# A two-layer graph network on one core: an addition at the ring's lap becomes a copy on ScalarE, and the last groups use four PSUM banks

## The chip, the cores and the metric

The kernel runs on one core of a Trainium2 chip. The metric is the device time of one execution in microseconds (us). The engines are named as in the profile: PE (TensorE), DVE (VectorE), ACT (ScalarE), POOL (GpSimd) and SP (SyncE, which here only issues DMAs).

## The reference

Two relational graph layers run over 12500 nodes and 200000 edges, sorted by destination, with 128 channels and 10 relations. An edge's relation is the argmax of 10 of its 42 attributes.

```
seg  = dst * 10 + edge_type
sums = segment_sum(x[src], seg)                     # one row per node and relation
mean = sums / max(count(seg), 1)
layer(x) = einsum('nrd,rdo->no', mean, w_rel) + x @ root + bias
h   = relu(layer1(x))
out = layernorm(x + layer2(h))
```

## The kernel before

**Tiles and gathers.** The 200000 edges are cut into 1563 tiles of 128. For each tile POOL issues one indirect DMA (`gathered`, L806), which fetches the source rows of its 128 edges into a slot of a buffer `g`. PE multiplies the gathered rows with a one-hot matrix `oh` (DVE makes it, ACT scales it by 1/count), and the product in PSUM (`zp`, L1058) holds the tile's contribution to a window of 12 nodes times 10 relations. DVE adds it to `cc` at an offset read at run time (`sum_into`, L844).

**The ring.** `cc` holds, per channel, two halves: `cc[:, 0]` the sums of layer 1, `cc[:, 1]` sums that layer 2 can already use, since a gather from tile NX = 177 on fetches two rows, x and the part of h that is finished (`XH`). Each half is a ring of RN = 1024 node columns per relation, and has EDGE = 172 more columns past its end, because windows overlap the end of a lap. Tile t covers nodes near 8 t. A window's offset is counted from the start of the lap in which its tile's lowest node lies, so sums past the end of the ring fall into the EDGE columns. `folded` (L786) is called by `finish` of the block that begins a lap: DVE adds the EDGE columns to the ring's first ones (L790) and sets them to zero (L791). There are twelve laps after the first, so twelve folds.

**Parts and blocks.** The program is written out in order, without loops on the chip. A part is four tiles. In step p of layer 1, DVE makes the one-hots of part p+2, ACT scales those of p+1, POOL gathers part p, DVE adds the products of part p-2, and PE multiplies part p. Four PSUM banks `zp` rotate, two tiles to a bank. From tile NX on a part takes one of four `g` buffers. When all tiles that can touch a block of nodes (256 nodes, at the end 128) are summed, `finish(k)` projects it: 20 matmul records with the relations' weights into `pf` (L799), then relu by ACT (`shifted`, L722). Then, spread over the following steps by `todo.at`, come the layer-2 messages of every node and relation: groups of four relations into the bank `yb` (L913), copied by ACT to one of two buffers `ys` (L919) and stored to `YD` by SP (L921). `cleared` (L772, ACT) zeroes the block's ring columns, and `sums_stored` (L778) writes the layer-2 half to `SD`. At the very end of layer 1 (`u = 0`) what is left runs at once.

**Layer 2** gathers 862 tiles from `YD`. The first eleven (tiles T0 to NX) read only the rows of early nodes; from the twelfth on a gather may read any row of `YD`. While these run, `brought_together` sorts the remaining edges with DVE passes over 127 rows of 1536 columns (`A`, `X`, `Y` lie in `cc`; `go` is a mask in PSUM); its last step before the lists are made sets entries of `A` without a flag to zero (L1262).

Of the kernel before, what the change touches and what calls it, by code (L numbers as in the profile page):

```python
# [9 lines left out]
F32 = mybir.dt.float32  # L10
BF16 = mybir.dt.bfloat16
I32 = mybir.dt.int32
AF = mybir.ActivationFunctionType
ALU = mybir.AluOpType
# [6 lines left out]
P = 128  # L21
# [4 lines left out]
KW = NREL * WN  # L26
WMAX = 120
G = 16
QB = 4
# [11 lines left out]
YB = 512  # L41
# [26 lines left out]
def rgcn_resnorm_kernel(ctx: ExitStack, tc: tile.TileContext, x, src, dst, attr, w_rel1, root1, b1,  # L68
# [151 lines left out]
    def next_of(kind, of):  # L220

        turn_of_[kind] += 1
        return of[(turn_of_[kind] - 1) % len(of)]
# [438 lines left out]
    def block(k):  # L662
        n0, n = ranges[-1][k]
        return n0, n, [(t, min(P, n - t * P)) for t in range(-(-n // P))]
# [117 lines left out]

    first_sum = starts[min(k for k in range(NBLK) if has_sums(k))]

    def folded(ls, k, w):

        if block(k)[0] % RN or not k:
            return
        s, e = cc[:, ls, :, :w], cc[:, ls, :, RN:RN + w]
        nc.vector.tensor_tensor(s, s, e, op=ALU.add)  # L790
        nc.vector.memset(e, 0.0)  # L791

    def projected(k, l, sums, w=None, f=None, po=None):

# [27 lines left out]
    def offsets(row, t0, n, limits, ring=True):  # L822

        lims = [limits(t0 + j) for j in range(n)]
        if ring:
            laps = [max(0, (t0 + j) * STEP - OFF) // RN * RN for j in range(n)]
            lims = [(lo - a, hi - a) for (lo, hi), a in zip(lims, laps)]
            assert all(hi + WN <= RW for _, hi in lims)
        vals = nc.values_load_multi_w_load_instructions(
            row, engines=[DVE], min_val=min(a for a, _ in lims), max_val=max(b for _, b in lims),  # L830
            skip_runtime_bounds_check_because="clamped to these nodes on the chip")[1]
        return [nc.s_assert_within(v, a, b, skip_runtime_bounds_check_because="clamped to these nodes on the chip")
                for v, (a, b) in zip(vals, lims)]

    def sum_into(ls, zp, at, off, w):

        m = NREL * w
        if ls.stop - ls.start == 2:
            s = cc[:, :, :, ds(off, w)]
            z = zp[:, at:at + 2 * m].rearrange("c (l r n) -> c l r n", r=NREL, n=w)  # L840
        else:
            s = cc[:, ls.start, :, ds(off, w)]
            z = zp[:, at:at + m].rearrange("c (r n) -> c r n", n=w)
        nc.vector.tensor_tensor(s, s, z, op=ALU.add)  # L844
# [39 lines left out]
    def layer_1():  # L884
# [6 lines left out]
        def finish(k, t):  # L891

            if k < NBLK - 2:
                todo.run(END)
            if k not in fTs:
                xbs[k] = rows_in(k)
                fTs[k] = features_in(k, 0, xbs[k])
            u = QB if t < NT else 0
            folded(ALL, k, EDGE)
            o = block(k)[0] % RN  # L900
            po = [projected(k, 0, cc[:, 0, :, o:o + block(k)[1]], rsb[0], fTs[k])]
            both = has_sums(k)
            reused = starts[k] + RN < N
            assert not reused or t + 7 * u <= (starts[k] + RN - OFF - WN) // STEP

            def rows_copied(_):
                a = po.pop()
                fin_a[k] = shifted(a, k, 0)

            def projected_rows(b, h, r):  # L910
                kept_rows()
                m = min(HB, NREL - r) * C
                nc.tensor.matmul(yb[:h, :m], fin_a[k][:, b * P:b * P + h], wsb[1][:, r:r + m // C, :], start=True, stop=True)  # L913
                unkept.append(lambda: projected_kept(b, h, r))

            def projected_kept(b, h, r):
                ys = next_of("ys", staged)
                m = min(HB, NREL - r) * C
                nc.scalar.activation(ys[:h, :m], yb[:h, :m], AF.Copy)  # L919
                n0 = block(k)[0] + 1 + b * P  # L920
                nc.sync.dma_start(by_node[n0:n0 + h, r * C:r * C + m], ys[:h, :m])  # L921
                if (b, r) == groups[-1][::2]:
                    fin_a.pop(k)

            def rows_out(_):
                a = fin_a[k]
                pr = ps_f.tile([P, 4, C], F32, name="pf")
                n0, n, subs = block(k)
                for i, h in subs:
                    nc.tensor.transpose(pr[:h, i, :], a[:, i * P:i * P + h], ident)  # L930
                po.append(pr)

            def rows_kept(_):
                pr = po.pop()
                hb = hbs.pop(k)
                for p, s in spans(k):
                    nc.scalar.activation(hb[:p, s, C:], pr[:p, s], AF.Copy)
                rows_dma(hb, XH[N:], k, True)

            def features_kept(_):  # L940
                n0, n, _ = block(k)
                nc.sync.dma_start(hT[:, n0:n0 + n], fin_a[k][:, :n])

            groups = [(b, h, r) for b, h in block(k)[2] for r in range(0, NREL, HB)]
            todo.at(t + u, rows_copied)
            if k <= K1:
                todo.at(t + 2 * u, rows_out)
                todo.at(t + 3 * u, rows_kept)
            else:
                hbs.pop(k, None)  # L950
            todo.at(t + 2 * u, features_kept)
            for j, (b, h, r) in enumerate(groups):
                i = 2 + j if k <= K1 else 1 + j
                todo.at(t + i * u, lambda _, b=b, h=h, r=r: projected_rows(b, h, r))
            todo.at(t + (i + 1) * u, kept_rows)
            if reused:
                todo.at(t + 2 * u, lambda t: cleared(0, k, 0))
                todo.at(t + 3 * u, lambda t: cleared(0, k, 1))
            if both:
                todo.at(t + u, lambda _: sums_stored(k))  # L960
            if k == NBLK - 1:
                todo.run(t)
                todo.run(END)
            if both:
                w = 10 if k >= NBLK - 3 else 5
                todo.at(t + w * u, lambda t: cleared(1, k, 0))
                todo.at(t + (w + 1) * u, lambda t: cleared(1, k, 1))
            if k + 1 < NBLK - 1:
                def fetch(t):
                    xbs[k + 1] = rows_in(k + 1)  # L970

                def turn(t):
                    n0, n, subs = block(k + 1)
                    pt = ps_f.tile([P, YB], F32, name="pf")
                    for i, h in subs:
                        nc.tensor.transpose(pt[:, i * P:i * P + h], xbs[k + 1][:h, i, :], ident[:h, :h])
                    po.append(pt)

                def turned_kept(t):
                    n0, n, subs = block(k + 1)  # L980
                    pt = po.pop()
                    fTs[k + 1] = fin.tile([P, 3 * P], F32, name="fT")
                    nc.scalar.activation(fTs[k + 1][:, :n], pt[:, :n], AF.Copy)
                todo.at(t + u, fetch)
                w = 2 if k == NBLK - 3 else 5
                todo.at(t + w * u, turn)
                todo.at(t + (w + 1) * u, turned_kept)
# [5 lines left out]
                unkept.pop()()  # L993

        fin_a = {}
        yb = ps_z.tile([P, YB], F32, name="yb")
        xbs[0] = rows_in(0)
        fTs[0] = features_in(0, 0, xbs[0])
        jobs = Later()
# [22 lines left out]
        for p in range(-AHEAD, NPT + BEHIND):  # L1022
# [38 lines left out]
            def sums(a, b):  # L1061
                nonlocal done, offs, row
                q = p - BEHIND
                if q < 0:
                    return
                t0, n = parts[q]
                if not a and t0 % CT == 0:
                    row = rows_.tile([1, CT], I32, name="row")
                    nc.scalar.dma_start(row, b_r[t0 // CT:t0 // CT + 1, :])
                if not a and t0 % G == 0:  # L1070
                    m = min(G, NT - t0)
                    offs = offsets(row[:, t0 % CT:t0 % CT + m], t0, m, bounds)
                for j in range(a, min(b, n)):
                    i = t0 + j
                    sum_into(ALL if i >= NX else ONE, zps[q, j // 2], j % 2 * 2 * KW, offs[i % G], WN)
                    if j % 2 or j == n - 1:
                        del zps[q, j // 2]
                if b < QB:
                    return
                while done < NBLK and t0 + n >= done_after(done):  # L1080
                    finish(done, t)
                    done += 1
# [65 lines left out]
    def brought_together(ready, first):  # L1148
# [108 lines left out]
        for a, b, t in ((0, KW, gl[:, :KW]), (KW, EW, go)):  # L1257
# [1 line left out]
            nc.vector.tensor_scalar(t, d0[:, a:b], LOW - 1, None, op0=ALU.bitwise_and)  # L1259
            nc.vector.tensor_scalar(q, t, -1.0, high[:NR], op0=ALU.mult, op1=ALU.add)  # L1260
            nc.vector.scalar_tensor_tensor(v[:, a:b], d0[:, a:b], 0.5, q, op0=ALU.is_gt, op1=ALU.mult)
        nc.vector.scalar_tensor_tensor(A, d0, 0.5, A, op0=ALU.is_gt, op1=ALU.mult)  # L1262
        yield 1
        n = -(-NT2 // P)
        assert sorted(first) == list(range(n))
# [501 lines left out]
```

## Time and profile before

| | |
|---|---|
| median of 3 runs | 3100.54 us (3100.3 to 3101.13) |
| profiled execution | 3102.92 us, its span 3101.1 us |
| granted TensorE clock, mean | 0.805 |
| indirect gathers on POOL | 2425 |
| first and last fold (L790) | 216.8 and 1987.8 us |
| last gather of layer 1, first of layer 2 | 1995.2 and 1996.4 us |
| last gather | 3083.1 us |

The page's first part gives the busy time of each engine. A line of the timeline has the start, the duration, the engine, the line of the code and the operation, and in brackets how long the engine was idle before it and what ended that. A line of a source view has the least, median and greatest duration in ns and the first and last start. A line of groups has the busy time, the mean duration in ns, and the idle time before.

### The profile page before, as it was taken

The page shows a single profiled execution, that of the slowest core. Times are in us where ns is not written, and L with a number is a line of the kernel's source. Part 1 is how long each engine was busy: PE and PEld are TensorE (multiplying, and loading weights), DVE is VectorE, ACT ScalarE, POOL GpSimd, SP SyncE. Part 2 cuts the span into 40 slices and gives each one's busy share as a digit, 9 for nine tenths or more (in the row PEclk, how much of TensorE's full clock was granted, in tenths as well). Part 3 has the DMA queues.
Part 4 walks back from the last instruction along what each step waited for, and adds up shares of the span by engine and source line. Part 5 has one row for each costly group of instructions (what it writes and reads, how often), then busy time and mean ns, then how long its engine had stood idle before and what let it go on. Part 6 is the DMA issues. An engine that isn't in the chain of part 4 may idle for free.

```text
span 3101.1 us, 42083 instructions
## 1 busy us (share of the span) xinstructions
PE 2228.4 (72%) x11120; PEld 1804.3 (58%) x11120; DVE 1703.7 (55%) x5058; ACT 1117.0 (36%) x3224; POOL 2335.1 (75%) x2437
## 2 busy tenths in 40 slices
PE   2777777877777878777778778755777777777554
PEld 1655666656665666666566656544566666666443
DVE  6665667867565747475657574468652323332332
ACT  3634434444444444444444444331221212221221
POOL 7777777777777777777777777777777777777775
PEclk7879888999888888999898999855777777777555
DMA  5755667675756676766666656632455555554222
GB/s 176 223 160 173 217 181 220 186 222 181 227 174 212 183 225 183 222 183 212 190 196 215 184 174 197 174 100 57 115 175 155 163 156 160 177 161 126 78 69 55
DMA packets 377358, 529.97 MB, mean 171 GB/s; under 512 B 56782, under 2 KB 284501, under 8 KB 377110
## 3 DMA queue, kind: packets, MB, share of 16 engines
q0 software_dynamic: 99776, 249.91, 29.0%
q1 hardware_dynamic: 249111, 264.44, 26.2%
q10 hardware_dynamic: 28223, 12.82, 1.4%
q8 instruction: 93, 1.52, 0.2%
q14 instruction: 155, 1.27, 0.1%
HBM read 373.17 MB, written 160.19 MB: 172 GB/s over the span
## 4 chain that ended last, share of the span: by engine, by line
PE 20%; DMA 19%; issue 7%; DVE 5%; POOL 2%; DVEq 0%; ACT 0%; SPq 0%; POOLq 0%; ACTq 0%
DMA g<-YD,idxB 10%; DMA g<-XH,idxE 8%; PE alone L799 8%; PE zp L1058 4%; POOL g L806 2%; PE zy L1560 2%; PE yb L913 2%; PE zq L1560 1%; PE pf L799 1%; PE pf L1284 1%; DVE cc L1589 1%; DVE cc L1252 1%; DMA cc<-hT 1%; DVE go L1240 0%; PE pf L1492 0%
## 5 line engine op out<-in xcount | busy, mean ns | idle before, releaser
L806 POOL DMA_INDIRECT g<-XH,idxE x1386 | 1344.9, 970 | 422.4 <-issue 200.2
L1058 PE MATMUL zp<-oh,g 128*128 128x120 f32 x5898 | 959.6, 308 | 432.7 <-DMA g<-XH,idxE 291.0
L1058 PEld LDWEIGHTS zp<-oh,g 128*128 128x128 f32 x5898 | 848.5, 213 | 656.7 <-DMA g<-XH,idxE 211.3
L844 DVE TENSOR_TENSOR cc<-cc,zp 128x240 f32 (+1 forms) x1563 | 607.0, 388 | 682.6 <-PE zp L1058 555.9
L806 POOL DMA_INDIRECT g<-YD,idxB x685 | 648.2, 946 | 208.7 <-issue 129.8
L812 ACT ACTIVATE oh<-oh,wE 128x120 f32<-128x120 f32 (+1 forms) x1740 | 522.0, 374 | 86.2 <-DVE oh L818 69.5
L1560 PE MATMUL zy<-oh,g 128*128 128x12 f32 (+22 forms) x1170 | 241.1, 329 | 229.5 <-DMA g<-YD,idxB 132.5
L1560 PEld LDWEIGHTS zy<-oh,g 128*128 128x128 f32 x1170 | 222.3, 265 | 262.3 <-DMA g<-YD,idxB 122.0
L919 ACT ACTIVATE ys<-yb 128x512 f32<-128x512 f32 (+2 forms) x294 | 154.4, 525 | 591.9 <-PE yb L913 571.6
L913 PE MATMUL yb<-w,a 128*128 128x512 f32 (+1 forms) x576 | 300.5, 608 | 5.5 <-ACT ys L919 5.5
L799 PE MATMUL alone<-cc,w 128*128 128x256 f32 (+2 forms) x920 | 293.8, 496 | 3.3 <-DVE cc L1482 3.3
L799 PEld LDWEIGHTS alone<-cc,w 128*128 128x128 f32 x920 | 236.4, 272 | 46.9 <-DVE cc L1482 3.5
L818 DVE TENSOR_TENSOR oh<-bank,keyE 128x480 f32<-128x480 f32 x391 | 253.2, 648 | 0.0
L799 PE MATMUL pf<-cc,w 128*128 128x256 f32 (+2 forms) x1040 | 246.6, 397 | 8.9 <-DVE cc L790 6.7
L799 PEld LDWEIGHTS pf<-cc,w 128*128 128x128 f32 x1040 | 206.6, 212 | 41.5 <-issue 8.7
L772 ACT ACTIVATE cc<-zero 128x1280 f32<-128x1280 f32 (+2 forms) x184 | 224.5, 1224 | 2.4 <-DVE tri L1178 2.4
L806 POOL DMA_INDIRECT g<-YD,idxE x177 | 169.4, 957 | 61.5 <-issue 36.9
L806 POOL DMA_INDIRECT g<-in_x_dram,idxE x177 | 171.0, 966 | 55.6 <-issue 34.7
L812 ACT ACTIVATE oh<-oh,wB 128x16 f32<-128x16 f32 (+27 forms) x685 | 159.8, 305 | 127.5 <-DVE cc L1589 62.1
L756 ACT ACTIVATE rstd<-mv,eps 128x2 f32<-128x2 f32 (+2 forms) x52 | 15.3, 295 | 521.8 <-DVE mv L754 521.7
L1560 PE MATMUL zq<-oh,g 128*128 128x16 f32 (+24 forms) x554 | 107.4, 313 | 97.8 <-DMA g<-YD,idxB 89.8
L1560 PEld LDWEIGHTS zq<-oh,g 128*128 128x128 f32 x554 | 96.9, 240 | 112.5 <-DMA g<-YD,idxB 80.1
(254 smaller groups left out, 1658.9 us busy)
## 6 DMA issues: line engine op xcount, KB each, us to landing
SD<-cc SPq DMA_DIRECT2D x41, 1280.0 KB
cc<-SD SPq DMA_DIRECT2D x41, 1280.0 KB
YD<-ys SPq DMA_DIRECT2D x194, 256.0 KB
m<-in_edge_attr_dram SPq DMA_DIRECT2D x48, 672.0 KB
g<-XH,idxE POOLq DMA_INDIRECT x1386
YD<-ys SPq DMA_DIRECT2D x97, 128.0 KB
XH<-hb SPq DMA_DIRECT2D x44, 256.0 KB
g<-YD,idxB POOLq DMA_INDIRECT x685
```

What stands on the lines that cost most here:

```text
L772: nc.scalar.activation(cc[:, l, h * H:(h + 1) * H, o:o + n], zero[:, None, :n].to_broadcast([P, H, n]), AF.Copy)
L799: nc.tensor.matmul(po[:, :n], wsb[l][:, r, :], sums[:, r], start=(r == 0), stop=(w is None and r == NREL - 1))
L806: nc.gpsimd.indirect_dma_start(out=g[:, j * C:(j + n) * C], out_offset=None, in_=table, in_offset=bass.IndirectOffsetOnAxis(ap=idx, axis=0))
L812: nc.scalar.activation(s, s, AF.Copy, scale=w)
L818: nc.vector.tensor_tensor(o.rearrange("p (t m) -> p t m", m=m), cols[:, None, :m].to_broadcast([P, n, m]), keys[:, :, None].to_broadcast([ ...
L844: nc.vector.tensor_tensor(s, s, z, op=ALU.add)
L913: nc.tensor.matmul(yb[:h, :m], fin_a[k][:, b * P:b * P + h], wsb[1][:, r:r + m // C, :], start=True, stop=True)
L919: nc.scalar.activation(ys[:h, :m], yb[:h, :m], AF.Copy)
L1058: nc.tensor.matmul(zp[:, o + l * KW:o + (l + 1) * KW], g[:, (slot[j] + l) * C:(slot[j] + l + 1) * C], oh[:, j * KW:(j + 1) * KW], start=Tr ...
L1252: nc.vector.copy_predicated(to[:, c - m:EW - m], go[:, c - KW:], a[:, c:])
L1284: nc.tensor.matmul(pp[:p, :2 * P], hot[:, j, :p], both[:, :, j * P:(j + 1) * P], start=(j == 0), stop=(j == m - 1))
L1560: nc.tensor.matmul(zp[:, j * w:(j + 1) * w], g[:, at * C:(at + 1) * C], oh[:, j * w:(j + 1) * w], start=True, stop=True)
```

## The change

`folded` and its call are gone. At the first tile of each lap ACT copies the EDGE columns over the ring's first ones (`lap_begun`), one half of `cc` before tile NX and both after it, and DVE zeroes the EDGE columns three parts later (`edge_cleared`). The messages of blocks finished at the end (`u = 0`) take their bank in turn from the four `zp` banks. Layer-2 ring columns that no later block reuses are no longer cleared. In `brought_together` ACT copies all but the first KW = 120 columns of `A` to the PSUM mask, and the last masking is split in two.

```
-    def folded(ls, k, w):
-        if block(k)[0] % RN or not k:
-            return
-        s, e = cc[:, ls, :, :w], cc[:, ls, :, RN:RN + w]
-        nc.vector.tensor_tensor(s, s, e, op=ALU.add)
-        nc.vector.memset(e, 0.0)
+    def lap_of_tile(t):
+        return max(0, t * STEP - OFF) // RN
+    def lap_begun(ls):
+        nc.scalar.activation(cc[:, ls, :, :EDGE], cc[:, ls, :, RN:], AF.Copy)
+    def edge_cleared(ls):
+        nc.vector.memset(cc[:, ls, :, RN:], 0.0)
...
     (finish)
-            folded(ALL, k, EDGE)
...
     (projected_rows)
+                yb = yb_ if u else next_of("zp", fixed)
...
-            if both:
-                w = 10 if k >= NBLK - 3 else 5
+            if both and reused:
+                w = 5
                 todo.at(t + w * u, lambda t: cleared(1, k, 0))
                 todo.at(t + (w + 1) * u, lambda t: cleared(1, k, 1))
...
     (sums, for each tile i of the part)
+                    if i and lap_of_tile(i) > lap_of_tile(i - 1):
+                        ls = ALL if i >= NX else ONE
+                        lap_begun(ls)
+                        todo.at(t + 3 * QB, lambda _, ls=ls: edge_cleared(ls))
                     sum_into(ALL if i >= NX else ONE, zps[q, j // 2], j % 2 * 2 * KW, offs[i % G], WN)
...
     (brought_together)
-        nc.vector.scalar_tensor_tensor(A, d0, 0.5, A, op0=ALU.is_gt, op1=ALU.mult)
+        ga = go.bitcast(F32)
+        nc.scalar.activation(ga, A[:, KW:], AF.Copy)
+        nc.vector.scalar_tensor_tensor(A[:, :KW], d0[:, :KW], 0.5, A[:, :KW], op0=ALU.is_gt, op1=ALU.mult)
+        nc.vector.scalar_tensor_tensor(A[:, KW:], d0[:, KW:], 0.5, ga, op0=ALU.is_gt, op1=ALU.mult)
```

More of the change, by code (lines that the diff above doesn't have):

```diff
@@ L825, in offsets @@
         if ring:
-            laps = [max(0, (t0 + j) * STEP - OFF) // RN * RN for j in range(n)]
+            laps = [lap_of_tile(t0 + j) * RN for j in range(n)]
             lims = [(lo - a, hi - a) for (lo, hi), a in zip(lims, laps)]
@@ L912, in projected_rows, with projected_kept @@
                 m = min(HB, NREL - r) * C
+                yb = yb_ if u else next_of("zp", fixed)
                 nc.tensor.matmul(yb[:h, :m], fin_a[k][:, b * P:b * P + h], wsb[1][:, r:r + m // C, :], start=True, stop=True)
-                unkept.append(lambda: projected_kept(b, h, r))
-            def projected_kept(b, h, r):
+                unkept.append(lambda: projected_kept(yb, b, h, r))
+            def projected_kept(yb, b, h, r):
                 ys = next_of("ys", staged)
@@ L995, in layer_1 @@
         fin_a = {}
-        yb = ps_z.tile([P, YB], F32, name="yb")
+        yb_ = ps_z.tile([P, YB], F32, name="yb")
         xbs[0] = rows_in(0)
```

## The prediction

> **What bounds the kernel now.** I read the page first, then the waits of POOL, then POOL's own timeline, and only then the other engines.
>
> ```profile
> span 3101.1 us, 42083 instructions
> PE 2228.4 (72%) x11120; PEld 1804.3 (58%) x11120; DVE 1703.7 (55%) x5058; ACT 1117.0 (36%) x3224; POOL 2335.1 (75%) x2437
> ```
>
> No engine looks full by its busy share. The waits of POOL tell more (who was waited for, total, times, longest):
>
> ```profile
> POOL g L806 <- issue: 401.6, 1318, 0.3
> POOL g L806 <- PE zp L1058: 149.6, 491, 0.3
> ...
> POOL g L806 <- DMA cc<-hT: 8.2, 2, 7.9
> ```
>
> Nearly every "wait" is 0.3 us long, whatever is named as its end: it is the fixed gap between two gathers. One is long, 7.9 us. So POOL issues one gather after another all the way through, and its pace is the time. The timeline of POOL and of DVE at one place where the ring folds shows the pace and what breaks it:
>
> ```profile
> 381.81 0.95 POOL L806 DMA_INDIRECT g<-XH,idxE  x1 [0.30 <-issue]
> 383.06 3.79 POOL L806 DMA_INDIRECT g<-XH,idxE  x1 [0.30 <-issue]
> 387.15 0.95 POOL L806 DMA_INDIRECT g<-XH,idxE  x1 [0.30 <-issue]
> 388.40 0.94 POOL L806 DMA_INDIRECT g<-XH,idxE  x1 [0.30 <-issue]
> ...
> 382.29 3.73 DVE L790 TENSOR_TENSOR cc<-cc 128x3440 f32<-128x3440 f32 x1
> 386.81 2.92 DVE L791 MEMSET cc<- 128x3440 f32 x1 [0.78 <-DVE cc L790]
> ```
>
> The pitch is 1.25 us (381.81 to 383.06): 0.95 busy and 0.30 gap. 2425 gathers at this pitch are 3031 us of the 3101. The gather issued during VectorE's addition L790 took 3.79 us and ended 0.83 us after the addition did (386.85 against 386.02). During the memset L791 (386.81 to 389.73) gathers took 0.95 and 0.94, so the memset costs POOL nothing. This happens at all twelve folds:
>
> ```profile
> L806 POOL DMA_INDIRECT g<-XH,idxE x1386: 942/947/4431, 229.1 to 1995.2; - x198
> L806 POOL DMA_INDIRECT g<-in_x_dram,idxE x177: 940/945/4479, 4.2 to 227.9; - x177
> ...
> L806 POOL DMA_INDIRECT g<-XH,idxE x1386 | 1344.9, 970 | 422.4 <-issue 200.2
> L806 POOL DMA_INDIRECT g<-in_x_dram,idxE x177 | 171.0, 966 | 55.6 <-issue 34.7
> ...
> L790 DVE TENSOR_TENSOR cc<-cc x12: 3733/3735/3742, 216.8 to 1987.8; 128x3440 f32<-128x3440 f32 x12
> L791 DVE MEMSET cc<- x12: 2925/2925/2925, 221.3 to 1992.4; 128x3440 f32 x12
> ...
> 216.85 4.48 POOL L806 DMA_INDIRECT g<-in_x_dram,idxE  x1 [0.30 <-DMA g<-in_x_dram,idxE]
> 1988.40 3.99 POOL L806 DMA_INDIRECT g<-XH,idxE  x1 [0.30 <-PE zp L1058]
> ```
>
> Twelve gathers take over 3.5 us, one inside each L790, the first and last of them shown; together 48.0 us. At 0.946 each they would take 11.4, so the folds lengthen POOL's work by **36.6 us**. The groups say the same: 1344.9 - 1386 x 0.947 = 32.4, and 171.0 - 177 x 0.945 = 3.7, together 36.1.
>
> **The change, part by part.** *The fold.* Gone are twelve additions (3.735 us) and twelve memsets (2.925 us, moved). POOL gains the 36.6 us, if each later gather follows at once. It does if its buffer is free; that is weighed below. The twelfth fold lies in the tail of layer 1: the late gather at 1988.40 is the last one that PE's chain of sums, projections and stores waits for before layer 2's full-table gathers, so the tail moves with it and the gain counts there too.
>
> *The copy at a lap.* ACT now copies 20 x 172 columns. ACT's clears are the nearest rows:
>
> ```profile
> L772 ACT ACTIVATE cc<-zero 128x1280 f32<-128x1280 f32 x172 | 216.7, 1261 | 0.0
> L772 ACT ACTIVATE cc<-zero 128x640 f32<-128x640 f32 x10 | 6.8, 726 | 0.0
> ```
>
> 640 columns more cost 0.535 us, 0.836 ns each, so 3440 columns take 1.261 + 2160 x 0.836 ns = 3.07 us (lap 1 copies one layer, 1720 columns: 1.63). ACT is 36% busy, and 172 clears of 1.26 us ran beside gathers none of which was long for it: the copy does not hold POOL. What it holds is DVE. The first sum of the lap waits for ACT, and ACT waits for the sum before: some 3.4 us with two hand-overs (an estimate: 3.07 and about 0.15 each). Behind that sum stand all later work of DVE and, in laps 3 to 9, the projection of the block before: the lap begins at tile 128 l + 10, and by the code's done_after that tile lies in the very part whose end releases that block. PE then waits too, with the products behind it, and a g buffer comes free later. How much room is there? Lap 3 has the least:
>
> ```profile
> 527.88 2.83 PE L1058 MATMUL zp<-oh,g 128*128 128x120 f32 x24
> ...
> 531.04 0.95 POOL L806 DMA_INDIRECT g<-XH,idxE  x1 [0.30 <-PE zp L1058]
> ```
>
> The gather of tile 416 at 531.04 reuses the buffer of tiles 400 to 403, whose last products are the first 8 of these 24, done at 528.8. That is 2.2 us of room, less than 3.4: a wait of about 1.3 us. The same count (start of a part's first gather less the end of the products four parts earlier) gives at least 3.5 us in lap 2, 5.0 in lap 7, and 5.9 and more in the other laps. The memset, three parts later, has 10 us and more of room except in lap 3 (3.3). So nothing in most laps, between 1 and 3 us in laps 2 and 3. I take **+2.0**; the bounds are 0 and 20 (about 1.7 us at every lap).
>
> *The mask L1262.* This also reads two tiles from SBUF:
>
> ```profile
> 2151.61 1.63 DVE L1261 SCALAR_TENSOR_TENSOR cc<-cc,go 127x1416 f32<-127x1416 int32 x1
> 2153.16 1.75 DVE L1262 SCALAR_TENSOR_TENSOR cc<-cc 127x1536 f32<-127x1536 int32 x1
> ...
> 2151.99 0.94 POOL L806 DMA_INDIRECT g<-YD,idxE  x1 [0.30 <-issue]
> 2153.23 2.49 POOL L806 DMA_INDIRECT g<-YD,idxE  x1 [0.30 <-issue]
> ```
>
> L1261, with its second input in PSUM (go), left a gather at 0.94; L1262, from SBUF alone, stretched one to 2.49. The change gives the long part the form of L1261, and leaves only 120 columns in the old form. **-1.5 us** for POOL. It costs 1.4 us of ACT (1416 columns by the rate above) that DVE waits for; DVE runs ahead of POOL there, no gather waits on DVE or PE in layer 2, so this is worth 0. If that cover were gone it would be +1.4.
>
> *The four banks.* The 7.9 us wait is that of the twelfth layer-2 gather, the first that reads the whole of YD and so must wait for layer 1's last row. The timelines of ACT, SP and PE there:
>
> ```profile
> 2008.95 0.94 POOL L806 DMA_INDIRECT g<-YD,idxE  x1 [0.30 <-issue]
> 2017.80 0.94 POOL L806 DMA_INDIRECT g<-YD,idxE  x1 [7.91 <-DMA cc<-hT]
> ...
> 2006.22 0.60 ACT L919 ACTIVATE ys<-yb 128x512 f32<-128x512 f32 x1 [0.57 <-PE yb L913]
> 2008.00 0.59 ACT L919 ACTIVATE ys<-yb 84x512 f32<-84x512 f32 x1 [1.18 <-PE yb L913]
> 2009.77 0.59 ACT L919 ACTIVATE ys<-yb 84x512 f32<-84x512 f32 x1 [1.18 <-PE yb L913]
> 2011.11 0.38 ACT L919 ACTIVATE ys<-yb 84x256 f32<-84x256 f32 x1 [0.75 <-PE yb L913]
> 2011.39 1.35 ACT L772 ACTIVATE cc<-zero 128x640 f32<-128x640 f32 x2
> 2012.65 0.37 ACT L919 ACTIVATE ys<-yb 128x256 f32<-128x256 f32 x1
> ...
> 2011.92 0.52 SPq L778 DMA_DIRECT2D SD<-cc  x1
> 2013.04 0.35 SPq L921 DMA_DIRECT2D YD<-ys  x1
> ...
> 2008.64 1.09 PE L913 MATMUL yb<-w,ae 128*84 128x512 f32 x2 [0.68 <-ACT ys L919]
> 2011.55 0.70 PE L913 MATMUL yb<-w,ad 128*128 128x256 f32 x2 [0.47 <-ACT ys L919]
> ```
>
> The name on the long wait (cc<-hT) is a neighbour that landed at that moment; the store of 2013.04 is what the gather needs. PE and ACT alternate on one bank: three waits like 0.68 and one of 0.47 go, and with the clears of blocks whose ring columns nobody reuses also the 0.40 between the last product (2012.25) and its copy: at most 2.9 us. But ACT writes into two staging buffers, and each must be stored before it is filled again. The one filled at 2008.00 was filled again at 2011.11 without a wait, so a store takes at most 2.5 us. By that bound the buffer filled at 2006.22 allows the next filling at 2009.3, and the last at 2012.4, against 2012.65: a gain of 0.25. Besides, the last store queues behind SD<-cc, which only moves with the copies. Between 0 and 2.9 I take **-0.7**, near the lower end, because these buffers and that queue stay. The stall cannot turn into something else: POOL is the next to be late. The last lap's memset falls between the sums of the last two parts, where DVE waits for PE anyway, and costs 0; without that cover it would be +2.9.
>
> Sum: -36.6 + 2.0 - 1.5 - 0.7 = **-36.8 us**. The profiled execution took 3102.92 (span 3101.1 and 1.8 around it), 2.4 over the median of 3100.54; the difference is carried to the median: **3063.7 us**. Layer 2, where POOL waits for nothing after 2017.80, only shifts.
>
> **The rivals.** *The lap's wait takes a third back.* If ACT is in the middle of another instruction when the last sum before a lap is done, 1.3 to 2.6 us (one or two clears) come on top of 3.4; against room of 5 to 9 us that gives POOL waits of 1 to 2 us at most laps: 12 to 20 us, so 3074 to 3082. For it: lap 3 is short already. Against: the ring's clears of the block before are issued well after the lap begins.
>
> *Slower: ACT is stuck behind a projection.* ACT waits for each projection before it can evict it:
>
> ```profile
> ACT a L722 <- PE pf L801: 304.6, 48, 15.2
> ```
>
> That is 304.6 / 48 = 6.3 us a time. Were the copy queued behind this at each lap, DVE would stand for 6.3 + 3.1 + 0.3 = 9.7 us and POOL, with some 5 us of room, for 4.7, less the fold's 3.05 saved: 12 x 1.65 = 20 us slower, 3118 with the other two terms. It decides above 8.1 us of standstill at every lap. Against: in program order the copy comes before the projection's eviction, not after it.
>
> *Nothing gained.* The long gathers would have another cause than L790's operands, or ACT's copy would stretch them just as well. Then the 36.6 stays, and the time is 3100.5 + 2.0 - 0.7 = 3101.8. Against: thirteen of thirteen operations from SBUF alone of over 1.7 us have their long gather, and L1261 and the clears have none. [...]
>
> **How the numbers follow.** Forecast 0.80 (3059.5 with both free terms at their best, to about 3070); the lap's wait 0.13; nothing gained 0.03; slower 0.04. The range 3059 to 3074 holds the first and the edge of the second. This kernel's measurements can tell about 0.2% (6.2 us) from no change; so faster 0.93, within 0.03, slower 0.04.
>
> **What would show it.** POOL's gathers in layer 1 have a longest of about 1.0 us, their mean falls from 970 to 947 ns; the long wait before the twelfth layer-2 gather stays, at about 7 us; L1262's gather is 0.95. Right or wrong on the lap: a POOL wait above 0.3 us near 128 l + 10 tiles, ACT's copy near 3.07 us, DVE idle before the lap's sum of about 3.4. Wrong altogether: gathers of 3 us that overlap ACT's copy or DVE's memset, or POOL waiting for PE in many laps.

## The result and the profile after

The changed kernel takes 3061.71 us (median of 4 runs, 3060.94 to 3062.05); beside it the kernel before took 3100.42 (3098.91 to 3101.13). The ratio is 0.9875 [0.9858, 0.9893]: faster by 38.7 us, where 36.8 had been forecast. The profiled execution took 3060.94 us with a span of 3059.2, at a granted clock of 0.807 (before: 0.805). Experiments 7, 9, 10 and 11 below ran on a chip on which the kernel before takes some 3709 us; their times are compared with each other only.

The page of after, its first part and its group of gathers:

```profile
PE 2219.6 (73%) x11120; PEld 1803.2 (59%) x11120; DVE 1659.3 (54%) x5047; ACT 1143.4 (37%) x3223; POOL 2295.3 (75%) x2437
...
L810 POOL DMA_INDIRECT g<-XH,idxE x1386 | 1310.6, 946 | 422.2 <-issue 199.5
```

The source view of its gathers:

```profile
L810 POOL DMA_INDIRECT g<-XH,idxE x1386: 942/946/988, 225.4 to 1957.0; - x198
L810 POOL DMA_INDIRECT g<-in_x_dram,idxE x177: 940/944/1107, 4.1 to 224.2; - x177
```

POOL's waits, and its timeline at the start of layer 2:

```profile
POOL g L810 <- PE zp L1062: 154.2, 506, 0.3
...
1970.76 0.94 POOL L810 DMA_INDIRECT g<-YD,idxE  x1 [0.30 <-issue]
1977.25 0.94 POOL L810 DMA_INDIRECT g<-YD,idxE  x1 [5.55 <-DMA cc<-hT]
```

(The changed code moves the lines: gathers L806 to L810, products L1058 to L1062, sums L844 to L848, messages L913 to L917 and their copies L919 to L923. The lap's copy is L791, its memset L795.) In layer 1 no gather is longer than 1.11 us; before, twelve took 3.6 to 4.5. POOL's busy time fell by 39.8 us and DVE's by 44.4, nearly the 44.8 of the twelve additions; ACT's rose by 26.4. POOL never waits for a product beyond its 0.3. One long wait remains, that of the twelfth gather of layer 2, 5.55 us in place of 7.91. The lap itself, in the timelines of ACT and DVE in lap 6:

```profile
991.62 3.07 ACT L791 ACTIVATE cc<-cc 128x3440 f32<-128x3440 f32 x1 [1.81 <-DVE cc L848]
...
994.73 0.84 DVE L848 TENSOR_TENSOR cc<-cc,zp 128x240 f32 x2 [1.44 <-ACT cc L791]
996.24 2.92 DVE L795 MEMSET cc<- 128x3440 f32 x1 [0.67 <-DVE cc L848]
```

ACT's copy takes the 3.07 us that the clears' rate gave, but DVE stands for 1.44 us, not 3.4. And lap 3, the one with the least room, in DVE's timeline (ACT's copy there runs from 512.03 to 515.10):

```profile
513.35 1.56 DVE L458 SCALAR_TENSOR_TENSOR reach<-u,reach 128x6 f32<-128x6 f32 x8
514.83 0.44 DVE L536 CAST d_f<-d_i 128x169 f32<-128x169 int32 x1
515.30 0.29 DVE L538 SCALAR_TENSOR_TENSOR k<-d_f,ty 128x128 f32<-128x128 f32 x1
...
516.04 0.84 DVE L848 TENSOR_TENSOR cc<-cc,zp 128x240 f32 x2
517.54 2.92 DVE L795 MEMSET cc<- 128x3440 f32 x1 [0.66 <-DVE cc L848]
```

Here DVE does not stand at all: preparations of later tiles lie in its queue between the sum that ACT waits for and the first sum of the lap, and they fill the copy's time.

### The profile page after: what moved, and what is told of

Read it like the earlier page. It is cut to its first block, busy times and chain, and to the rows that moved or that the text cites. A ratio compares the mean times of both kernels' runs of the same rounds, so it can differ in the third digit from the quotient of the medians.

```text
span 3059.2 us, 42098 instructions
## 1 busy us (share of the span) xinstructions
PE 2219.6 (73%) x11120; PEld 1803.2 (59%) x11120; DVE 1659.3 (54%) x5047; ACT 1143.4 (37%) x3223; POOL 2295.3 (75%) x2437
## 4 chain that ended last, share of the span: by engine, by line
DMA 24%; PE 22%; issue 8%; DVE 7%; POOL 3%; ACT 1%; DVEq 0%; SPq 0%; POOLq 0%; ACTq 0%
DMA g<-XH,idxE 13%; DMA g<-YD,idxB 10%; PE alone L803 7%; PE zp L1062 6%; POOL g L810 3%; PE zy L1571 2%; PE yb L917 2%; PE pf L803 1%; DVE cc L848 1%; PE zq L1571 1%; PE pf L1295 1%; DVE cc L1600 1%; DVE cc L1260 1%; DMA cc<-hT 1%; DVE go L1248 1%
## 5 line engine op out<-in xcount | busy, mean ns | idle before, releaser
L810 POOL DMA_INDIRECT g<-XH,idxE x1386 | 1310.6, 946 | 422.2 <-issue 199.5
L1062 PE MATMUL zp<-oh,g 128*128 128x120 f32 x5898 | 964.6, 309 | 404.1 <-DMA g<-XH,idxE 250.1
L1062 PEld LDWEIGHTS zp<-oh,g 128*128 128x128 f32 x5898 | 857.3, 215 | 628.4 <-DVE cc L848 206.0
L848 DVE TENSOR_TENSOR cc<-cc,zp 128x240 f32 (+1 forms) x1563 | 607.1, 388 | 687.9 <-PE zp L1062 552.1
L810 POOL DMA_INDIRECT g<-YD,idxB x685 | 647.7, 946 | 208.8 <-issue 134.4
L923 ACT ACTIVATE ys<-yb 128x512 f32<-128x512 f32 (+1 forms) x291 | 152.4, 524 | 539.2 <-PE yb L917 515.0
L917 PE MATMUL yb<-w,a 128*128 128x512 f32 (+1 forms) x576 | 304.5, 615 | 6.4 <-ACT ys L923 6.4
L803 PE MATMUL pf<-cc,w 128*128 128x256 f32 (+2 forms) x1040 | 232.4, 381 | 4.1 <-DVE cc L848 4.1
L772 ACT ACTIVATE cc<-zero 128x1280 f32<-128x1280 f32 x170 | 214.3, 1261 | 0.0
L803 PEld LDWEIGHTS pf<-cc,w 128*128 128x128 f32 x1040 | 195.2, 200 | 32.0 <-DVE cc L848 5.4
L810 POOL DMA_INDIRECT g<-YD,idxE x177 | 167.9, 949 | 59.2 <-issue 36.6
L810 POOL DMA_INDIRECT g<-in_x_dram,idxE x177 | 167.4, 946 | 55.5 <-issue 33.2
```

Source lines behind the costliest of these rows:

```text
L772: nc.scalar.activation(cc[:, l, h * H:(h + 1) * H, o:o + n], zero[:, None, :n].to_broadcast([P, H, n]), AF.Copy)
L803: nc.tensor.matmul(po[:, :n], wsb[l][:, r, :], sums[:, r], start=(r == 0), stop=(w is None and r == NREL - 1))
L810: nc.gpsimd.indirect_dma_start(out=g[:, j * C:(j + n) * C], out_offset=None, in_=table, in_offset=bass.IndirectOffsetOnAxis(ap=idx, axis=0))
L1062: nc.tensor.matmul(zp[:, o + l * KW:o + (l + 1) * KW], g[:, (slot[j] + l) * C:(slot[j] + l + 1) * C], oh[:, j * KW:(j + 1) * KW], start=Tr ...
```

## The experiments

**1. The lap's copy alone.** Into the kernel before go only `lap_begun`, `edge_cleared` and their calls, and `folded` goes; banks, clears and mask stay as they were.

> The kernel before with the lap's copy alone: ScalarE copies at the lap, the addition is gone; one bank for the last groups, all clears and the undivided mask stay. If the fold's additions are what held POOL, no gather of layer 1 is over 1.2 us, and the gain is 36.6 us and a little for PE's tail, 37 to 39 us: 3062 to 3064. The one gather beside the undivided mask is still near 2.5 us. Rival: the fold is only one of several causes and the other three edits bring a good part; then this is above 3070.

3064.77 us (3063.79 to 3067.58) beside 3101.35: ratio 0.9879 [0.9864, 0.9894], that is -36.6 us where 37 to 39 had been expected; the interval is some 4.6 us to each side. No gather of layer 1 is long; the mask's gather still takes 2.50 us.

**2. All but the copy.** The reverse: the changed kernel with `folded` in place of the copy.

```
-    lap_begun(ls)
-    todo.at(t + 3 * QB, lambda _, ls=ls: edge_cleared(ls))
+    folded(ALL, k, EDGE)          # in finish, as before
```

> The change without the lap's copy: the fold's addition and memset are back at their place, the four banks, the clears left out and the divided mask stay. By the theory the twelve long gathers are back (sum about 48 us), the gather beside the mask is near 0.95, the long wait before the twelfth layer-2 gather is 0.5 to 1 us under 7.9, and the time is 1.5 + 0.7 = 2 us under before: 3098, ratio 0.9993. Rival: the two edits at the end of layer 1 bring the 2.4 us by which that wait became shorter; then 3096 to 3097 and a wait of 5.5 us.

3098.49 (3097.11 to 3102.26), ratio 0.9992 [0.9983, 1.0001]. The twelve long gathers are back. The two source lines of its gathers:

```profile
L810 POOL DMA_INDIRECT g<-XH,idxE x1386: 940/946/4443, 228.8 to 1992.7; - x198
L810 POOL DMA_INDIRECT g<-in_x_dram,idxE x177: 940/944/4424, 4.2 to 227.6; - x177
```

So the copy is nearly all of the change. The two halves add up within the noise (-36.6 and -2.9 against -38.7), and the interval of this half by itself reaches no change. The long wait of the tail is 8.16 us here; neither the theory (0.5 to 1 under 7.9) nor the rival (5.5) had that.

**3. The copy on DVE.** Is it the engine or the operands that count? The lap's copy is given to DVE.

```
-        nc.scalar.activation(cc[:, ls, :, :EDGE], cc[:, ls, :, RN:], AF.Copy)
+        nc.vector.tensor_copy(cc[:, ls, :, :EDGE], cc[:, ls, :, RN:])
```

> The changed kernel with the lap's copy on VectorE (one input in SBUF, output in SBUF, 3440 columns) in place of ScalarE. If only an operation with two inputs in SBUF holds a gather, none is over 1.2 us and the time stays at 3061 to 3064. Rival: a copy from SBUF to SBUF on VectorE holds it as well; then up to twelve gathers end 0.82 us after the copy does, and with a copy of 1.9 to 3.6 us the time is 15 to 35 us longer, 3076 to 3097. [...]

3077.27 (3076.95 to 3077.5), ratio 0.9921 [0.9905, 0.9936]: the copy holds gathers too, though it reads a single tile. Twelve gathers take 1.5 to 2.5 us, 15.2 too much together. POOL's and DVE's timelines at two of the laps:

```profile
677.44 2.28 POOL L810 DMA_INDIRECT g<-XH,idxE  x1 [0.31 <-PE pf L275]
...
676.95 1.96 DVE L791 COPY cc<-cc 128x3440 f32<-128x3440 f32 x1
...
833.73 2.10 POOL L810 DMA_INDIRECT g<-XH,idxE  x1 [0.30 <-DMA g<-XH,idxE]
...
833.72 1.99 DVE L791 COPY cc<-cc 128x3440 f32<-128x3440 f32 x1
```

The first gather began inside the copy and ended 0.81 us after it (679.72 against 678.91), as beside the addition. The second began within 0.01 us of the copy's start and ended 0.12 after it (835.83 against 835.71). So these two held gathers ended at different distances from the copy's end, 0.81 and 0.12 us. Beside the addition only the first was seen, 0.81 to 0.86 us. The copy took 1.96 and 1.99 us at these laps; the 1.9 to 3.6 expected of it was an estimate, not read off a run.

**4. The addition in 20 pieces.** In the kernel before, one addition for each half and relation, 172 columns each.

```
-        nc.vector.tensor_tensor(s, s, e, op=ALU.add)
+        for l in range(2):
+            for r in range(NREL):
+                nc.vector.tensor_tensor(s[:, l, r], s[:, l, r], e[:, l, r], op=ALU.add)
```

> The kernel before with each fold's addition cut into 20 additions of 172 columns, one for each layer and relation, one behind the other; the memset stays whole. If a gather waits only for the instruction that runs when it starts, it is held at most 0.3 us, and some 4 gathers fall into each fold: excess under 1 us a fold, 12 at most in all, time 3066 to 3076. Rival: POOL is held for the whole run of additions; then each fold costs the length of the run, 5 to 7 us, and the time is 3120 to 3150.

3081.62 (3078.36 to 3086.74), ratio 0.9931 [0.9916, 0.9946]: neither theory. The timelines of POOL and DVE at one fold:

```profile
868.94 0.99 POOL L808 DMA_INDIRECT g<-XH,idxE  x1 [0.30 <-PE yb L915]
870.24 4.16 POOL L808 DMA_INDIRECT g<-XH,idxE  x1 [0.30 <-PE zp L1060]
...
868.54 5.04 DVE L792 TENSOR_TENSOR cc<-cc 128x172 f32<-128x172 f32 x20
```

The gather at 868.94 passed among the pieces, the one at 870.24 was held through all that were left and ended 0.82 after the last (874.40 against 873.58). In seven of the twelve folds a gather was held so, for 3.4 to 4.2 us; in five all passed. In those seven a row of short additions, each behind the other, thus acted like one long one. What decides which gather passes is open: of those held and of those that passed, some began at the same point of a piece (0.21 us into it).

**5. The addition twice.** The kernel before, with a second addition (of the zeroes) after the memset.

```
         nc.vector.memset(e, 0.0)
+        nc.vector.tensor_tensor(s, s, e, op=ALU.add)
```

> The kernel before with a second addition of the same 3440 columns behind each fold's memset (it adds zeros). If each such addition holds the one gather that starts in it until 0.82 us after its end, there are 24 long gathers, some 3 us more each: 36 us slower than before, 3134 to 3140. Rival: POOL has room of its own that takes up part of it, or the cost is a fixed one for each fold; then under 3120.

3133.37 (3131.04 to 3139.89), ratio 1.0102 [1.0086, 1.0119], just under the expected span. POOL and DVE at one fold:

```profile
391.62 0.94 POOL L807 DMA_INDIRECT g<-XH,idxE  x1 [0.30 <-PE zp L1059]
392.87 3.42 POOL L807 DMA_INDIRECT g<-XH,idxE  x1 [0.30 <-issue]
...
388.77 2.92 DVE L791 MEMSET cc<- 128x3440 f32 x1 [0.78 <-DVE cc L790]
391.73 3.74 DVE L792 TENSOR_TENSOR cc<-cc 128x3440 f32<-128x3440 f32 x1
```

Each second addition holds one gather for 3.42 us, 2.48 too long; twelve make 29.8 of the 32.6 us. It is less than 3.05 a fold because the gather that began 0.11 us before the addition passed, and the held one began only 1.14 us into it.

**6. The copy twice.** The changed kernel; ACT makes the lap's copy two times in a row.

> The changed kernel with each lap's copy done twice on ScalarE, one behind the other, so that VectorE gets the lap's first sum 3.1 us later. If the copy costs nothing because the gather buffers leave room (least 0.5 us in lap 3, 4.5 us and more elsewhere in the changed kernel's trace), only lap 3 makes POOL wait, some 2.6 us: 3062 to 3066. Rival: the wait at a lap is paid in full whatever the room; then 11 x 3.1 = 34 us, 3096.

3063.61 (3061.33 to 3069.0), ratio 0.9878 [0.9861, 0.9894] against the change's 0.9875: nothing to be told apart. POOL's waits for products and the one of the tail:

```profile
POOL g L811 <- PE zp L1063: 154.6, 507, 0.3
...
POOL g L811 <- DMA cc<-hT: 8.5, 2, 8.2
```

With 6.1 us of copy POOL still waits nowhere at a lap. The least room fell to 0.1 us (tile 548, lap 4), so this is about the limit; the wait of 2.6 us that had been expected in lap 3 did not come.

**7 and 9. A transfer without a list.** What in a gather is held? Behind each gather of some tiles POOL issues a plain transfer from DRAM to DRAM (`pl`), which reads no indices: in the kernel before around each fold (7), and in experiment 3's kernel around each lap (9). Both kernels do this extra work, so their times are not used.

```
     gathered(g, slot[j], XH[:N + limit_of(i)], idx, 2)
+    if 30 <= i % CT < 62:           # in 9: 10 <= i % CT < 42
+        nc.gpsimd.dma_start(next_of("pl", plains), x[:P, :16])
```

> The kernel before with a plain DMA on POOL's queue (128 rows of 16 columns from DRAM to DRAM, no index list) behind each gather, for 32 tiles around each fold. They lengthen the run by some 1.2 us each (about 350 of them, 400 us); only the durations beside the folds matter. If the addition holds a gather at the reading of its index list, a plain DMA that starts inside an addition keeps its usual duration, and gathers that start inside one still end 0.82 us after it. [...]

> The same plain DMAs around each lap in the kernel that copies on VectorE. [...] Rival: a plain DMA passes beside the copy as beside the addition.

The source view of the plain transfers in 7, then POOL and DVE at a fold:

```profile
L1048 POOL DMA_DIRECT2D pl<-in_x_dram x333: 587/587/610, 295.4 to 2367.2; - x167
...
707.95 0.59 POOL L1048 DMA_DIRECT2D pl<-in_x_dram  x1
708.85 2.78 POOL L807 DMA_INDIRECT g<-XH,idxE  x1 [0.30 <-issue]
...
707.03 3.73 DVE L791 TENSOR_TENSOR cc<-cc 128x3440 f32<-128x3440 f32 x1
```

The same of 9, at a lap:

```profile
L1052 POOL DMA_DIRECT2D pl<-in_x_dram x337: 585/587/1887, 433.3 to 2507.6; - x169
...
2493.11 1.89 POOL L1052 DMA_DIRECT2D pl<-in_x_dram  x1
...
2492.73 2.14 DVE L792 COPY cc<-cc 128x3440 f32<-128x3440 f32 x1
```

Six plain transfers began 0.36 to 0.91 us into an addition, and all took 587 to 595 ns, as usual; the gather behind each was held and ended 0.86 us after the addition. All three that began inside a copy took 1.88 to 1.89 and ended 0.12 us after it, so the rival of 9 falls. Gathers that had begun before a copy could be held in 9 too: three that began 0.25 to 0.54 us before it ended 0.12 after it, and one that began 0.08 before it ended 0.86 after. In experiment 3 one that began 0.54 us before the copy passed, with 0.95 us; what decides is open. So the addition held gathers and none of the six plain transfers, and the copy held both. In the code a gather has a list of indices, `idxE`, in SBUF, and a plain transfer has none. That the reading of this list is what the addition holds is my guess: it agrees with experiments 3, 5, 7 and 9, does not say why some gathers pass in 4, and is shown by no run. What a held plain transfer waits for was not shown either.

**8. The last groups in other buffers.** The changed kernel; the last block's groups are written to idle one-hot buffers in place of the two `ys`, and the last store of `SD` goes behind the last row's.

```
-                ys = next_of("ys", staged)
+                ys = next_of("ys", staged) if u else next_of("oh", hots_)
...
-                todo.at(t + u, lambda _: sums_stored(k))
+                todo.at(t + u if u else END, lambda _: sums_stored(k))
```

> The changed kernel; the groups of the last block are staged in one-hot buffers that are idle by then, in place of the two staging buffers, and the last block's sums are stored to SD behind its last row. If the store of the staging buffers and the store ahead in the queue are what is left of the wait before the twelfth layer-2 gather, ScalarE no longer waits for a store there, the last row is stored about 3 us earlier, and the wait falls from 5.5 to about 2 us: 3057 to 3059. Rival: the wait is set by when PE reaches the last groups; then it stays at 5 us or more and so does the time.

3059.05 (3056.44 to 3060.85), ratio 0.9863 [0.9846, 0.9879]. From the first product of the last groups to the last store it now takes 4.28 us (7.32 in the changed kernel), and the long wait is 3.43, where about 2 had been expected. The intervals of the two ratios overlap, so a gain over the change is likely and not established.

**10 and 11. Without the last memset.** On the chip named above, the changed kernel (10), and experiment 8's kernel without the memset of the twelfth lap, whose columns nobody reads again (11).

```
-    todo.at(t + 3 * QB, lambda _, ls=ls: edge_cleared(ls))
+    if lap_of_tile(i) < lap_of_tile(NT - 1):
+        todo.at(t + 3 * QB, lambda _, ls=ls: edge_cleared(ls))
```

> The changed kernel as it is, for comparison with the next on one chip: 3061 to 3063. All theories expect the same.

> The kernel with the last groups staged in idle one-hot buffers and the last sums stored behind the last row, and besides without the memset of the twelfth lap, which nobody needs. If the memset delays the last sums, as in the changed kernel's trace (VectorE went from it to the sum without a pause), the last projection starts about 0.6 to 1 us earlier and the wait before the twelfth layer-2 gather is 2 to 3 us: 3057 to 3059, 3 us under the changed kernel. Rival: PE's own chain sets it, then this equals the kernel with staging alone, 3059, and the wait stays near 3.4 us.

3707.95 and 3707.68 us beside 3709.18 for the kernel before: ratios 0.9999 [0.9983, 1.0015] and 0.9997 [0.9982, 1.0012]. Here the whole change gains nothing that these runs can tell. The page's group of gathers and two of the waits, of 10:

```profile
L810 POOL DMA_INDIRECT g<-XH,idxE x1386 | 1313.9, 948 | 763.3 <-issue 294.0
...
POOL g L810 <- remote: 337.4, 257, 4.7
...
POOL g L810 <- PE zp L1062: 213.1, 186, 32.7
```

A gather lasts as long as in the first profile of after (948 ns, there 946), but POOL idles 763.3 us before these gathers (422.2 in the first profile of after). It waits for PE's products, once for 32.7 us, where none of these waits was over 0.3 in the first profile of after, and for 337.4 us for what the profile names "remote" only. So here POOL does not issue without a pause. That shorter gathers only lengthened its idle time is the likely reading; the kernel before was not profiled on this chip. The granted clock was 0.737 here, against 0.807; whether that, or what else, makes this chip slow stays open.

**12. The same, on another chip.** Experiment 11's kernel once more.

> The change with two additions: the last block's four groups are written to idle one-hot buffers instead of the two staging buffers, and the memset of the twelfth lap, whose columns nobody reads again, is left out. Theory (the last block is bound by the two staging buffers and, ahead of it, by that memset): the twelfth lap's memset of 2.92 us no longer stands ahead of the last sum on VectorE, which starts 0.5 to 1 us earlier; the last store falls some 3 to 4 us after the chain's start as with the staging buffers alone, and the time is 3055 to 3060, some 2 to 4 below the change's 3061.7. Rival (the memset is hidden and the end is set by how late the products reach the last groups): as with the staging buffers alone, 3057 to 3061. The two are hard to tell apart by the time alone; the start of the last sum after the last product decides.

3060.84 (3060.45 to 3062.63) beside 3104.56: ratio 0.9859 [0.9842, 0.9875]. PE's and ACT's timelines of the tail, and POOL's long wait:

```profile
1963.56 1.50 PE L1062 MATMUL zp<-oh,g 128*128 128x120 f32 x12
1966.05 2.46 PE L803 MATMUL pf<-cc,w 128*128 128x84 f32 x20
...
1970.53 0.59 ACT L923 ACTIVATE oh<-zp 84x512 f32<-84x512 f32 x1 [0.26 <-PE zp L917]
1971.39 0.86 ACT L923 ACTIVATE oh<-zp 84x512 f32<-84x512 f32 x2 [0.26 <-PE zp L917]
1972.25 0.38 ACT L923 ACTIVATE ys<-yb 128x256 f32<-128x256 f32 x1
...
1976.71 0.94 POOL L810 DMA_INDIRECT g<-YD,idxE  x1 [1.75 <-issue]
```

ACT now waits only 0.26 us for PE and for no store, and POOL's wait is 1.75 us. By the test that was set for it the rival holds: the last sums begin 1.09 us after the start of their products here, and 1.09 in experiment 8, which has the memset. The shorter wait comes with earlier groups: they begin 8.3 us after layer 1's last gather here and 10.0 in 8. The lowest ratios of all are those of 8 and 12, which have no difference between them that these runs can tell; both lie within the change's interval.

## Why the prediction was right, and where it was not

**The fold, -36.6: right in size, and in that the addition is the cause.** Experiment 1 measures -36.6 for this part alone; experiment 2 shows that without it the gain is gone, experiment 5 that a second addition has its price again. Two inputs are no condition, though: experiment 3's copy reads one tile and holds gathers too (1.5 to 2.5 us), on DVE and not on ACT (at most 1.11 in layer 1 of after). Where POOL did not issue without a pause (experiment 10, ratio 0.9999) there was no gain.

**The lap, +2.0: wrong, it is 0.** The step that failed is "What it holds is DVE", with its standstill of 3.4 us: I took the copy's whole time as DVE's loss. The trace of after shows DVE standing 0 to 2.1 us before the lap's sum in eleven laps, because other work of DVE lies between the two sums (lap 12, with 5.5, is below). The least room left is 0.5 us (lap 3), but that is one execution: in experiment 8, with the same copy, it was 2.2 there. The memset was misplaced too: in laps 3 to 9 it does not come three parts later but directly behind the lap's first sums, as at 517.54 above, because the end of a block runs all that is still waiting in `todo`, due or not. It cost nothing there. The rival of a wait at most laps falls further with experiment 6, where twice the copy brings no wait.

**The mask, -1.5: right.** POOL's and DVE's timelines of after:

```profile
2114.10 1.02 POOL L810 DMA_INDIRECT g<-YD,idxE  x1 [0.30 <-issue]
...
2114.03 0.28 DVE L1272 SCALAR_TENSOR_TENSOR cc<-cc 127x120 f32<-127x120 int32 x1
2115.53 1.63 DVE L1273 SCALAR_TENSOR_TENSOR cc<-cc,go 127x1416 f32<-127x1416 int32 x1 [1.23 <-ACT go L1271]
```

The gather takes 1.02 in place of 2.49. DVE waits 1.23 us for ACT, and no gather waits for that.

**The banks, -0.7: right in size, and for the reason given.** ACT's and SP's timelines of after:

```profile
1969.43 0.59 ACT L923 ACTIVATE ys<-zp 84x512 f32<-84x512 f32 x1 [1.24 <-DMA YD<-ys]
1970.65 0.38 ACT L923 ACTIVATE ys<-zp 84x256 f32<-84x256 f32 x1 [0.63 <-DMA YD<-ys]
1972.56 0.38 ACT L923 ACTIVATE ys<-yb 128x256 f32<-128x256 f32 x1 [1.52 <-DMA YD<-ys]
...
1971.46 0.52 SPq L778 DMA_DIRECT2D SD<-cc  x1
1972.96 0.35 SPq L925 DMA_DIRECT2D YD<-ys  x1
```

ACT waits for the stores of the two buffers, and PE's groups, over in 3.64 us (1965.64 to 1969.28) where they had taken 7.12, no longer matter. From their first product to the last store it is 7.32 us after 7.91 before: 0.59. The four kernels with one bank (before, 1, 4 and 5) all have 7.91 or 7.92 here, the four with four banks and two buffers (after, 2, 3 and 6) 6.99 to 7.77. With the buffers out of the way (experiment 8) it is 4.28. The long wait itself fell by 2.36, to 5.55, and not to about 7. Of that 1.31 is no effect of the banks but of how late PE arrives: its last groups began 8.62 us after layer 1's last gather here, 9.93 before, and between 8.3 and 15.7 in experiments 1 to 6, 8 and 12, which is not explained. The other 0.47 lies between the last store and the gather.

**The last memset, 0: right in experiment 8, 0.5 in after.** I put it where DVE waits for PE. In this execution of after it ran into the last sums (PE's and DVE's timelines):

```profile
1960.12 1.50 PE L1062 MATMUL zp<-oh,g 128*128 128x120 f32 x12
...
1963.12 2.46 PE L803 MATMUL pf<-cc,w 128*128 128x84 f32 x20 [0.64 <-DVE cc L848]
...
1958.93 2.92 DVE L795 MEMSET cc<- 128x3440 f32 x1 [0.67 <-DVE cc L848]
1961.77 1.29 DVE L848 TENSOR_TENSOR cc<-cc,zp 128x240 f32 x3
```

From the last products' start to the last projection it is 3.00 us; without this memset, in experiment 12, 2.49 (1963.56 to 1966.05). But in experiment 8, with the memset, it is 2.50 as well: there the products came later, and DVE still waited 0.98 us for them behind the memset.

**The sum.** -36.6 + 0 - 1.5 - 0.6 is -38.7, and the medians differ by 38.7. The agreement to the last digit is luck: the interval of the ratio is some 5 us to each side, the memset's 0.5 is not in the sum, and the two profiled spans, in which the long wait fell by 2.36, differ by 41.9. One gather of layer 2 stays long, 1.71 us at 1997.22: it ends 0.82 us after another DVE operation on tiles in SBUF (L1216, 1.62 us), which the change leaves as it is.

**The other rivals.** "Nothing gained" falls with experiments 1 and 2. "Slower" did not come either. Before eleven of the twelve copies ACT was free when DVE's last sum was done, and began 0.03 to 0.04 us after it; before ten of them it had been idle, as for 1.81 us in lap 6 above, 10.3 us in all. At lap 12 what this rival describes did happen. The last sum there ended at 1944.16, but ACT was waiting for a projection, and four scalings of one-hots came next (ACT's timeline):

```profile
1945.20 0.37 ACT L722 ACTIVATE a<-pf,b 128x128 f32<-128x128 f32 x1 [1.73 <-PE pf L805]
...
1946.60 3.06 ACT L791 ACTIVATE cc<-cc 128x3440 f32<-128x3440 f32 x1
```

The copy came 2.44 us late and DVE stood for 5.53. It cost POOL nothing, as no gather had less than 8.4 us of room there.

## What to carry to other kernels

Look for the engine that issues without a pause, whatever its busy share (POOL had 75% here), and then for its few long instructions: what another engine does at that moment is the first suspect, and both ends, compared to the hundredth of a microsecond, tell whether they go together (0.83 us apart in the kernel before). The wait that this edit added cost DVE only what its queue could not fill in the meantime, in eleven laps 0 to 2.1 us of a copy of up to 3.07, so read what stands between the two instructions before pricing such a wait. And the gain on POOL was worth nothing on the chip of experiment 10 (ratio 0.9999), where POOL idled 763.3 us before the layer's gathers in place of 422.2: read the idle time first.

## What the runs showed of the hardware

I had not expected three things. A DVE copy from SBUF to SBUF, with one input, held POOL's gathers (to 0.81 to 0.86 us after its end, or to 0.12 for some that had begun between 0.54 us before it and 0.01 into it) and its plain transfers (to 0.12), while an addition of two SBUF tiles held gathers (to 0.81 to 0.86 after its end) and none of six plain transfers. Twenty additions of 0.33 us in a row held a gather so that it took as long as 4.16 us, although none of them is longer than a gather (0.95). And one chip ran the same kernels a fifth slower (3709 us against 3100), at the same mean duration of gathers (948 ns against 946) and a granted clock of 0.737 against 0.807, with 337.4 us of POOL's waits that the profile names "remote" only.
